# A three-layer graph attention kernel: tiles of nodes taken from the last to the first, and dense pieces placed between the edge steps

## The chip, the cores and the metric

The kernel runs on one core of one Trainium2 chip. The metric is device time in microseconds (us) of one execution, smaller is better. The engines that matter are TensorE (PE, with its weight loads as PEld), VectorE (DVE), ScalarE (ACT), GpSimd (POOL), and the queue of SyncE (SP) for plain DMAs.

## What is computed

There are 4096 nodes with 512 features, and an adjacency matrix of 4096 x 4096 zeros and ones. Its chance of an edge falls with both node numbers, as 1/sqrt((i+1)(j+1)), so the first nodes have many edges and the last few. The reference, shortened:

```python
def gat(x, mask, W, a):                 # heads of one layer
    Wh = einsum('nf,hfo->hno', x, W)
    e = leaky_relu(src(Wh, a)[:, :, None] + dst(Wh, a)[:, None, :], 0.2)
    e = where(mask, e, -huge)
    return einsum('hnm,hmo->hno', softmax(e), Wh)

x  = layernorm(x + gat(x, mask, W0, a0))          # layer 0, 8 heads of 64
h  = elu(gat(x, mask, W1, a1))                    # layer 1, 8 heads of 64
h  = elu(gat(h, mask, Wo, ao))                    # layer 2, 1 head of 512
h  = relu(h @ lin1_w + lin1_b) @ lin2_w + lin2_b  # dense, 512 -> 1024 -> 512
out = layernorm(x + h)
```

All arithmetic is in float32.

## The kernel before

Nodes are cut into 32 tiles (`NT`) of 128 (`P`). The kernel first searches the edges of each tile and packs them, in `find_edges`: the result is, per tile, a number of chunks of 128 edges. Each half of a tile (64 nodes) has chunks of its own, so that a pair of chunks serves both halves. Beside the search, `beside` projects the tile for layer 0. The chunk counts are fixed when the program is built: tile 0 has 55 (in four parts), tile 1 has 22, then 17, 15, 14, 12, 12, 11, four tiles of 10, ten of 8, one of 7, and tiles 23 to 31 have 6. That is 339 in all, 284 without tile 0.

A layer reads a table in DRAM with one row per node: 512 projected features and the scores of its heads. `attend(pools, st, t)` walks over the chunks of one tile in steps of up to `GC = 3` pairs. A step does this:

- one gather on POOL for each chunk (L880, indirect DMA of 128 rows into the tile `g`);
- the nodes' own scores by a matmul with the packed selection (pss, L890), summed by DVE into `s` (L898);
- `z` from `s` and the gathered scores, leaky relu, less the part for the shift (L904 to L908, DVE);
- weights by two exponentials on ACT (`w`, L910, and `wp` in PSUM, L916);
- in layers 0 and 1, the gathered rows times `wp` in place (L918, DVE), and a 0/1 selection `sm` (L919); in layer 2 one `sm` per chunk that holds the weight (L927);
- matmuls on PE that add the rows up by node (`acc`) and the weights (`den`), L939.

Buffers: `g` has six steps in layers 0 and 1 and four in layer 2; `acc` has two, `den` one, `pss` two in layers 0 and 1 and one in layer 2.

In `heads_layer` (layers 0 and 1) `after(sums, t)` finishes a tile: `o` is acc over den (L977), then `finish` (layer 0: residual, layernorm, row stored; layer 1: elu), then `project` makes the rows of the next layer's table: transposes `pt` (L631), copy to `xt` (ACT, L633), the sums `xpart` (DVE, L638) that are added to `xsum` on POOL (L639), the product `ph` (L642) and the scores `pa` (L645), and the row written out (`hrow`, L622 and L623, stored by SP). `project_end` closes the table with a row for nodes without edges, so the first gather of the next layer comes after the last projection. The loop goes over tiles 0 to 31, and `after` of a tile stands behind the whole `attend` of the next one.

Layer 2 has `fold` in place of `after` (acc over den, elu, transposes, a column of `sht`, L1047 to L1057). Four tiles make a block (`NJ = 4`). `first_dense(b, ks)` does two of eight slices of the first dense layer of a block (L1065, ACT relu L1068), `second_dense(b, j)` the second dense layer and the layernorm of one tile (p2, L1077, one PSUM buffer; L1080, L955 to L961) and stores it. In each turn of the loop over t, after the `fold` of tile t-1, the kernel does one piece of `first_dense` of the block before and one `second_dense` of the block before that.

The order of the instructions on each engine isn't the order of the text. The tile framework puts them in order when the program is built, with the order of the text as the priority and its own estimates of when operands are ready; it also places the waits. Each engine then works through its own list.

Of the kernel before, what the change touches and what calls it, by code (L numbers as in the profile page):

```python
# [24 lines left out]
NT = N // P  # L25
NB = 512
NBLK = N // NB
NJ = NB // P
# [4 lines left out]
HC = HID // P  # L33
# [6 lines left out]
GC = 3  # L40
# [489 lines left out]
def sparse_path(  # L530
# [24 lines left out]
    pts = parts()  # L555
# [39 lines left out]
    st0 = Stage2("t0", 8, 64, dest_first=False)  # L595
# [29 lines left out]

    def project(sb, ps, st, proj, src, t, smalls=1):
        w_sb, wa = proj
# [5 lines left out]
        nc.scalar.copy(xt, pt)  # L633
        if t == 0:
            nc.vector.tensor_reduce(st.xsum, xt, AX.X, OP.add)
        else:
            part = sb.tile([P, FC], F32, name="xpart")
            nc.vector.tensor_reduce(part, xt, AX.X, OP.add)  # L638
            nc.gpsimd.tensor_add(st.xsum, st.xsum, part)  # L639
# [222 lines left out]

    def attend(pools, st, t):

        gp, wk, pacc, ps = pools
        hs = st.heads
        acc = pacc.tile([P, F], F32, name="acc")
        den = pacc.tile([P, hs], F32, name="den", bufs=1)
        runs = []
        for p in pts:  # L870
            if p.t == t:
                small = min(p.chunks)
                for a, b, hn in ((0, small, 2), (small, p.pairs, 1)):
                    runs += [(p.first + lo, min(GC, b - lo), hn) for lo in range(a, b, GC)]
        seen, left = [0, 0], [sum(m for _, m, hn in runs if hn > h) for h in range(2)]
        for c0, m, hn in runs:
# [19 lines left out]
            n = m * hn  # L896
# [33 lines left out]
            for i in range(m):  # L930
# [3 lines left out]
                for out_, rows in (  # L934
# [3 lines left out]
                    for h in range(hn):  # L938
# [5 lines left out]
                        )  # L944
        return acc, den

# [16 lines left out]
    def heads_layer(st, nxt, proj_of, finish):  # L963
        with ExitStack() as pools:
# [6 lines left out]
            ps = pools.enter_context(tc.tile_pool(name=f"hp_{st.name}", bufs=1, space=PSUM))  # L971
            def after(sums, t):
                acc, den = sums
                o = sb.tile([P, F], F32, name="o")
# [8 lines left out]
                finish(sb, o, t)  # L983
                project(sb, ps, nxt, proj, o, t, 2)


            acc = attend((gp, wk, pacc, ps), st, 0)
            for t in range(1, NT):
                ahead, acc = acc, attend((gp, wk, pacc, ps), st, t)
                after(ahead, t - 1)  # L990
            after(acc, NT - 1)
            project_end(sb, ps, nxt, proj, 2)
# [12 lines left out]
    with ExitStack() as pools:  # L1005
# [7 lines left out]
        def beside(t):  # L1013
            xr = sb.tile([P, F], F32, name="xr")
            nc.sync.dma_start(xr, x[ts(t, P), :])
            project(sb, ps, st0, proj, xr, t)

# [8 lines left out]
    with tc.tile_pool(name="tb", bufs=1) as big, tc.tile_pool(name="tg", bufs=4) as gp, \  # L1026
# [14 lines left out]
        nc.sync.dma_start(l2b, lin2_b.partition_broadcast(P))  # L1041
        hts, hids = {}, {}

        def fold(sums, t):
            acc, den = sums
            rd = sb.tile([P, 1], F32, name="rd")
# [5 lines left out]
            for c in range(FC):  # L1052
                nc.tensor.transpose(pt[:, c, :], o[:, ts(c, P)], ident)
            b, j = divmod(t, NJ)
            if j == 0:
                hts[b] = big.tile([P, FC, NB], F32, name="sht", bufs=2)
            nc.scalar.copy(hts[b][:, :, ts(j, P)], pt)  # L1057

        def first_dense(b, ks):
# [10 lines left out]
        def second_dense(b, j):  # L1070
            t = b * NJ + j
            xr = sb.tile([P, F], F32, name="xr")
# [12 lines left out]

        acc = None
        for t in range(NT + 2 * NJ + 1):
            ahead, acc = acc, attend((gp, wk, pacc, ps), st, t) if t < NT else None
            if ahead is not None:
                fold(ahead, t - 1)  # L1090
            b, j = divmod(t - 1, NJ)
            if 1 <= b <= NBLK:
                first_dense(b - 1, range(j * HC // NJ, (j + 1) * HC // NJ))
            if 2 <= b:
                second_dense(b - 2, j)

# [55 lines left out]
```

## Time and profile before

| what | value |
|---|---|
| three runs, us | 2890.80, 2912.05, 2925.34; median 2912.05 |
| profiled execution, us | 2625.14, span 2623.2 |
| mean granted TensorE clock | 0.849 |
| edge search, with layer 0's projection | 0 to 692 us of the span |
| layer 0 | 692 to 1300 |
| layer 1 | 1300 to 1855 |
| layer 2 | 1855 to 2623 |
| gathers | 1017, POOL busy 1.01 us each |
| HBM traffic | 371.00 MB read, 42.23 MB written |

The profiled execution is one run by itself with the hardware profiler on. Every stage and duration comes from it, and it is shorter than the three runs. Rows of the profile name a line of the kernel, the engine, the operation, and the tiles written and read. "Busy" is the time in which an engine has an instruction at work; the granted clock is the share of the full clock that PE was given.

### The profile page before, as it was taken

Reading aid. Unit: us, or ns where it says so; the run is one execution under the profiler, and the core shown is the slowest. Engines: PE = TensorE matmul, PEld = TensorE weight load, DVE = VectorE, ACT = ScalarE, POOL = GpSimd, SP = SyncE. Lnnn points to the kernel's source line nnn. Section 1 sums busy time; section 2 is a strip of 40 time slices with the busy share of each in tenths; the row PEclk is TensorE's granted clock in tenths of the full one; section 3 lists DMA queues with packets and bytes.
Section 4 is the critical chain, followed back from the end, with each engine's and each line's share of the span. In section 5 each row is a group of like instructions: output and inputs, shape, how many; then the busy total and the mean of one; then the engine's idle time right before and its main releaser. Section 6 shows DMA issues by size and latency. Waiting matters only on the chain.

```text
span 2623.2 us, 28047 instructions
## 1 busy us (share of the span) xinstructions
PE 2001.1 (76%) x8501; PEld 891.6 (34%) x8501; DVE 1617.4 (62%) x5141; ACT 509.5 (19%) x919; POOL 1082.8 (41%) x1276
## 2 busy tenths in 40 slices
PE   2125788999467777777647777887567899999997
PEld 0002333334123333333312333443233444444443
DVE  5998777888666777766556777776234334443322
ACT  1001223333001222222101111222000123232320
POOL 3000000000177775563067776771577744453000
PEclk9556668999678888888867898999787999999999
DMA  5002244654277886674167787782677754454111
GB/s 172 0 33 80 95 151 161 227 200 180 70 204 236 244 247 190 198 237 143 68 172 205 217 219 193 202 220 79 210 201 202 201 155 146 139 164 132 57 36 46
DMA packets 138071, 415.21 MB, mean 158 GB/s; under 512 B 33515, under 2 KB 33523, under 8 KB 133814
## 3 DMA queue, kind: packets, MB, share of 16 engines
q0 software_dynamic: 81360, 269.62, 36.9%
q1 hardware_dynamic: 56550, 143.70, 15.5%
q8 instruction: 70, 1.15, 0.2%
q14 instruction: 91, 0.75, 0.1%
HBM read 371.00 MB, written 42.23 MB: 158 GB/s over the span
## 4 chain that ended last, share of the span: by engine, by line
PE 50%; DVE 22%; DMA 9%; issue 8%; POOL 7%; ACT 2%; POOLq 0%; SPq 0%; DVEq 0%; ACTq 0%
PE ph L642 13%; PE acc L939 11%; DMA g<-table_t,idx 8%; PE p L1065 8%; PE p L1077 8%; POOL g L880 6%; DVE g L918 5%; DVE cand L737 4%; PE pa L645 3%; PE key L731 2%; PE key L730 2%; DVE cand L754 1%; PE pt L631 1%; DVE lst L752 1%; ACT xt L633 1%
## 5 line engine op out<-in xcount | busy, mean ns | idle before, releaser
L880 POOL DMA_INDIRECT g<-table_t,idx x1017 | 1027.4, 1010 | 569.8 <-issue 278.0
L939 PE MATMUL acc<-g,sm 128*64 128x512 f32 x2034 | 618.9, 703 | 141.4 <-DVE g L918 127.6
L642 PE MATMUL ph<-sw_t,xt 128*128 128x512 f32 x768 | 456.2, 727 | 46.1 <-ACT xt L633 46.1
L918 DVE TENSOR_TENSOR g<-g,wp 128x3072 f32<-128x3072 f32 (+4 forms) x156 | 384.4, 2464 | 14.5 <-ACT wp L916 14.2
L939 PEld LDWEIGHTS acc<-g,sm 128*64 128x64 f32 x2034 | 159.0, 157 | 359.2 <-issue 150.6
L1065 PE MATMUL p<-sht,sl1w 128*128 128x512 f32 x512 | 234.4, 601 | 0.7 <-ACT sht L1057 0.7
L642 PEld LDWEIGHTS ph<-sw_t,xt 128*128 128x128 f32 x768 | 158.3, 227 | 216.9 <-issue 150.4
L1077 PE MATMUL p<-sl2w,shid 128*128 128x512 f32 x512 | 225.4, 593 | 3.7 <-DVE xr L1080 3.7
L639 POOL TENSOR_TENSOR xsum_t<-xsum_t,xpart 128x4 f32<-128x4 f32 x93 | 20.3, 218 | 487.4 <-DVE xpart L638 312.7
L737 DVE MAX8 cand<-key 128x8 f32<-128x353 f32 (+55 forms) x467 | 204.3, 447 | 22.2 <-PE key L731 21.9
L904 DVE TENSOR_TENSOR z<-s,g 128x48 f32<-128x48 f32 (+8 forms) x234 | 42.3, 184 | 220.5 <-DMA g<-table_t,idx 217.2
L721 ACT ACTIVATE sg<-raw 128x4096 bf16<-128x4096 int32 x32 | 115.7, 3617 | 218.8 <-PE key L730 211.5
L910 ACT ACTIVATE w<-z 128x48 f32<-128x48 f32 (+8 forms) x234 | 50.2, 220 | 522.3 <-DVE z L908 504.3
L730 PE MATMUL key<-sg,s_identb 128*128 128x512 bf16 (+1 forms) x258 | 114.2, 443 | 48.2 <-DVE cand L737 19.3
L1077 PEld LDWEIGHTS p<-sl2w,shid 128*128 128x128 f32 x512 | 97.0, 190 | 127.5 <-issue 120.5
L622 ACT COPY hrow<-ph 128x512 f32<-128x512 f32 (+1 forms) x99 | 57.8, 584 | 379.1 <-PE ph L642 331.4
L1065 PEld LDWEIGHTS p<-sht,sl1w 128*128 128x128 f32 x512 | 91.7, 190 | 93.3 <-issue 91.9
L645 PEld LDWEIGHTS pa<-swa_t,xt 128*128 128x128 f32 x768 | 108.4, 209 | 42.6 <-issue 30.5
L757 POOL COPY over<-lst 128x1 f32<-128x1 f32 x35 | 6.5, 187 | 275.6 <-DVE lst L752 247.4
L890 PE MATMUL pss<-s_t,s 128*128 128x48 bf16 (+1 forms) x543 | 49.0, 181 | 87.3 <-DVE s L898 82.2
L939 PEld LDWEIGHTS den<-w,sm 128*64 128x64 f32 x1356 | 67.5, 149 | 138.9 <-ACT w L910 63.9
L731 PE MATMUL key<-frac,ones_b 64*128 64x512 bf16 (+1 forms) x258 | 114.6, 444 | 0.0
(132 smaller groups left out, 2240.3 us busy)
## 6 DMA issues: line engine op xcount, KB each, us to landing
raw<-in_adj_dram SPq DMA_DIRECT2D x32, 2048.0 KB, 8.0
table_t<-hrow SPq DMA_DIRECT2D x64, 260.0 KB, 2.1
xr<-in_x_dram SPq DMA_DIRECT2D x64, 256.0 KB, 4.4
g<-table_t,idx POOLq DMA_INDIRECT x1017, 4.0
table_t<-hrow SPq DMA_DIRECT2D x32, 256.5 KB, 4.3
sx_d<-o SPq DMA_DIRECT2D x32, 256.0 KB, 4.5
xr<-sx_d SPq DMA_DIRECT2D x32, 256.0 KB, 2.6
out_dram<-xr SPq DMA_DIRECT2D x32, 256.0 KB
```

The lines of the kernel that those rows point to most:

```text
L622: nc.scalar.copy(hrow[:n, :F], ph[:n].rearrange("p h d -> p (h d)"))
L642: nc.tensor.matmul(ph, xt[:, c, :], w_sb[:, c], start=(c == 0), stop=(c == FC - 1))
L645: nc.tensor.matmul(pa, xt[:, c, :], wa[:, c], start=(c == 0), stop=(c == FC - 1))
L721: nc.scalar.activation(sg, raw, AF.Sign)
L730: nc.tensor.matmul(key[:, j - w0_ : e - w0_], ident_b, sg[:, j:e], start=True, stop=False)
L731: nc.tensor.matmul(key[:, j - w0_ : e - w0_], ones_b, frac[:, j:e], start=False, stop=True)
L737: nc.vector.max(out=cand[:, at : at + 8], in_=part)
L880: nc.gpsimd.indirect_dma_start(out=g[:, i, h, :], out_offset=None, in_=st.table[:, :], in_offset=bass.IndirectOffsetOnAxis(ap=idx[:, c0 + ...
L918: nc.vector.tensor_mul(body, body, wp[:, :, :, None].to_broadcast([P, n, hs, st.dim]))
L939: nc.tensor.matmul(out_[h * HN : (h + 1) * HN], sm[:, i * hn + h], rows[h], start=first[h], stop=seen[h] == left[h],)
L1065: nc.tensor.matmul(p1, l1w[:, c, ts(k, P)], hts[b][:, c, :], start=(c == 0), stop=(c == FC - 1))
L1077: nc.tensor.matmul(p2, hids[b][:, k, ts(j, P)], l2w[:, k, :], start=(k == 0), stop=(k == HC - 1))
```

## The change

Five things change.

1. `attend` becomes a generator that yields after each step, with the number of gathers in it; it leaves `acc` and `den` in a dictionary.
2. A tile's steps get even sizes: pairs are cut into equal parts rather than threes and a rest. The number of steps stays 78. Four pairs become 2+2 in place of 3+1.
3. In layers 0 and 1 the tiles go from 31 to 0, and `after` of the tile before comes behind the first step of a tile, not behind its last. The first tile of the order, and not tile 0, sets `xsum`.
4. In layer 2 the order is 31, 30, 29, 28, 27, 0, 26, ... 1. Blocks are made of four tiles that follow each other in this order; the first has 24 gathers.
5. Dense pieces go into a list when the last tile of their block is folded: four pieces of `first_dense` and four of `second_dense`. From the second block on, each gather adds 64/315 to what is due, and after a step as many pieces are done as are due and ready. What is left is done at the end.

```diff
--- before.py
+++ after.py
@@ -623,7 +623,7 @@
         nc.vector.tensor_copy(hrow[:n, F:], pa[:n, 1, :])
         nc.sync.dma_start(st.table[lo : lo + n, :], hrow[:n, :])
 
-    def project(sb, ps, st, proj, src, t, smalls=1):
+    def project(sb, ps, st, proj, src, t, first, smalls=1):
         w_sb, wa = proj
         hs, dm = st.heads, st.dim
         pt = ps.tile([P, FC, P], F32, name="pt")
@@ -631,7 +631,7 @@
             nc.tensor.transpose(pt[:, c, :], src[:, ts(c, P)], ident)
         xt = sb.tile([P, FC, P], F32, name="xt")
         nc.scalar.copy(xt, pt)
-        if t == 0:
+        if first:
             nc.vector.tensor_reduce(st.xsum, xt, AX.X, OP.add)
         else:
             part = sb.tile([P, FC], F32, name="xpart")
@@ -860,18 +860,27 @@
         nc.vector.tensor_copy(flag, pf[:1])
 
 
-    def attend(pools, st, t):
-
-        gp, wk, pacc, ps = pools
-        hs = st.heads
-        acc = pacc.tile([P, F], F32, name="acc")
-        den = pacc.tile([P, hs], F32, name="den", bufs=1)
+    def runs_of(t):
+
         runs = []
         for p in pts:
             if p.t == t:
                 small = min(p.chunks)
                 for a, b, hn in ((0, small, 2), (small, p.pairs, 1)):
-                    runs += [(p.first + lo, min(GC, b - lo), hn) for lo in range(a, b, GC)]
+                    steps = math.ceil((b - a) / GC)
+                    cuts = [a + (b - a) * i // steps for i in range(steps + 1)] if steps else []
+                    runs += [(p.first + i, j - i, hn) for i, j in zip(cuts, cuts[1:])]
+        return runs
+
+    def attend(pools, st, t, sums):
+
+
+        gp, wk, pacc, ps = pools
+        hs = st.heads
+        acc = pacc.tile([P, F], F32, name="acc")
+        den = pacc.tile([P, hs], F32, name="den", bufs=1)
+        sums[t] = acc, den
+        runs = runs_of(t)
         seen, left = [0, 0], [sum(m for _, m, hn in runs if hn > h) for h in range(2)]
         for c0, m, hn in runs:
             g = gp.tile([P, GC, 2, st.row], F32, name="g")[:, :m, :hn]
@@ -942,7 +951,7 @@
                             rows[h],
                             start=first[h], stop=seen[h] == left[h],
                         )
-        return acc, den
+            yield n
 
     def elu(sb, t):
         ex = sb.tile([P, F], F32, name="ex")
@@ -969,8 +978,10 @@
             sb = pools.enter_context(tc.tile_pool(name=f"hs_{st.name}", bufs=2))
             pacc = pools.enter_context(tc.tile_pool(name=f"ha_{st.name}", bufs=2, space=PSUM))
             ps = pools.enter_context(tc.tile_pool(name=f"hp_{st.name}", bufs=1, space=PSUM))
-            def after(sums, t):
-                acc, den = sums
+            sums = {}
+
+            def after(t):
+                acc, den = sums.pop(t)
                 o = sb.tile([P, F], F32, name="o")
                 rd = sb.tile([P, HS], F32, name="rd")
                 nc.vector.reciprocal(rd, den)
@@ -981,14 +992,18 @@
                     op=OP.mult,
                 )
                 finish(sb, o, t)
-                project(sb, ps, nxt, proj, o, t, 2)
-
-
-            acc = attend((gp, wk, pacc, ps), st, 0)
-            for t in range(1, NT):
-                ahead, acc = acc, attend((gp, wk, pacc, ps), st, t)
-                after(ahead, t - 1)
-            after(acc, NT - 1)
+                project(sb, ps, nxt, proj, o, t, t == order[0], 2)
+
+
+
+            order = list(range(NT - 1, -1, -1))
+            ahead = None
+            for t in order:
+                for step, _ in enumerate(attend((gp, wk, pacc, ps), st, t, sums)):
+                    if step == 0 and ahead is not None:
+                        after(ahead)
+                ahead = t
+            after(ahead)
             project_end(sb, ps, nxt, proj, 2)
 
     def finish0(sb, o, t):
@@ -1013,7 +1028,7 @@
         def beside(t):
             xr = sb.tile([P, F], F32, name="xr")
             nc.sync.dma_start(xr, x[ts(t, P), :])
-            project(sb, ps, st0, proj, xr, t)
+            project(sb, ps, st0, proj, xr, t, t == 0)
 
         find_edges(big, sb, ps, pk, constants, beside)
         project_end(sb, ps, st0, proj)
@@ -1039,10 +1054,15 @@
         nc.vector.tensor_copy(l1b, pb)
         l2b = big.tile([P, F], F32, name="sl2b")
         nc.sync.dma_start(l2b, lin2_b.partition_broadcast(P))
-        hts, hids = {}, {}
-
-        def fold(sums, t):
-            acc, den = sums
+
+
+        order = list(range(NT - 1, 0, -1))
+        order.insert(NJ + 1, 0)
+        blocks = [order[i : i + NJ] for i in range(0, NT, NJ)]
+        hts, hids, sums, ready = {}, {}, {}, []
+
+        def fold(t):
+            acc, den = sums.pop(t)
             rd = sb.tile([P, 1], F32, name="rd")
             nc.vector.reciprocal(rd, den)
             o = sb.tile([P, F], F32, name="o")
@@ -1051,10 +1071,14 @@
             pt = ps.tile([P, FC, P], F32, name="pt")
             for c in range(FC):
                 nc.tensor.transpose(pt[:, c, :], o[:, ts(c, P)], ident)
-            b, j = divmod(t, NJ)
+            b, j = divmod(order.index(t), NJ)
             if j == 0:
                 hts[b] = big.tile([P, FC, NB], F32, name="sht", bufs=2)
             nc.scalar.copy(hts[b][:, :, ts(j, P)], pt)
+            if j == NJ - 1:
+                per = HC // NJ
+                ready.extend((first_dense, b, range(i * per, (i + 1) * per)) for i in range(NJ))
+                ready.extend((second_dense, b, i) for i in range(NJ))
 
         def first_dense(b, ks):
             if 0 in ks:
@@ -1068,7 +1092,7 @@
                 nc.scalar.activation(hids[b][:, k, :], p1, AF.Relu, bias=l1b[:, k : k + 1])
 
         def second_dense(b, j):
-            t = b * NJ + j
+            t = blocks[b][j]
             xr = sb.tile([P, F], F32, name="xr")
             nc.sync.dma_start(xr, x1_d[ts(t, P), :])
             nc.vector.tensor_add(xr, xr, l2b)
@@ -1083,16 +1107,23 @@
 
 
 
-        acc = None
-        for t in range(NT + 2 * NJ + 1):
-            ahead, acc = acc, attend((gp, wk, pacc, ps), st, t) if t < NT else None
-            if ahead is not None:
-                fold(ahead, t - 1)
-            b, j = divmod(t - 1, NJ)
-            if 1 <= b <= NBLK:
-                first_dense(b - 1, range(j * HC // NJ, (j + 1) * HC // NJ))
-            if 2 <= b:
-                second_dense(b - 2, j)
+        head = sum(sum(p.chunks) for p in pts if p.t in blocks[0])
+        rate_ = 2 * NT / (sum(sum(p.chunks) for p in pts) - head)
+        due, ahead = 0.0, None
+        for t in order:
+            for step, chunks in enumerate(attend((gp, wk, pacc, ps), st, t, sums)):
+                if step == 0 and ahead is not None:
+                    fold(ahead)
+                if t not in blocks[0]:
+                    due += chunks * rate_
+                while due >= 1 and ready:
+                    due -= 1
+                    piece, *what = ready.pop(0)
+                    piece(*what)
+            ahead = t
+        fold(ahead)
+        for piece, *what in ready:
+            piece(*what)
 
 
 @with_exitstack
```

## The prediction, made before the changed kernel ran

> **What bounds the kernel now.** I read the page's busy shares first, then a table of stages (windows cut where the gathers of each layer begin), then the timeline of one repeating period in layers 0 and 1. No engine is full over the span, so the stages have to be read one by one.
>
> ```profile
> span 2623.2 us, 28047 instructions
> PE 2001.1 (76%) x8501; PEld 891.6 (34%) x8501; DVE 1617.4 (62%) x5141; ACT 509.5 (19%) x919; POOL 1082.8 (41%) x1276
> ...
> L880 POOL DMA_INDIRECT g<-table_t,idx x1017 | 1027.4, 1010 | 569.8 <-issue 278.0
> ```
> ```profile
> 0.00:692.00 692.00, 463.12 (x1422) 186.84 (x1423) 560.37 (x2395) 153.24 (x97) 41.70 (x197) 0.74 0.35 124
> 692.00:1300.00 608.00, 440.36 (x2198) 200.67 (x2195) 402.53 (x898) 111.99 (x284) 349.25 (x370) 0.82 0.65 194
> 1300.00:1855.00 555.00, 416.27 (x2208) 186.66 (x2206) 371.11 (x801) 85.18 (x255) 351.14 (x371) 0.87 0.68 186
> 1855.00:2095.00 240.00, 167.07 (x883) 90.16 (x885) 92.99 (x429) 24.59 (x69) 183.99 (x183) 0.85 0.72 207
> 2095.00:2623.20 528.20, 514.32 (x1803) 227.26 (x1798) 190.43 (x618) 134.53 (x214) 156.71 (x156) 0.99 0.38 110
> ```
> Columns: window, length, busy us and instructions of PE, PEld, DVE, ACT, POOL, granted clock, DMA share, GB/s. Row 1 is the edge search, which the change leaves as it is. Rows 2 and 3 are layers 0 and 1. Rows 4 and 5 are layer 2: 240 us paced by gathers while PE works 167, then PE without a gap.
>
> A gather takes POOL 1.00 us and 0.30 us of issue, 1.30 us in a row; a layer has 339 of them, 441 us. Layers 0 and 1 last longer than that, and PE (440, 416) and DVE (403, 371) don't fill them either. What sets the small tiles is a chain that goes round between the engines. Layer 0, tiles of eight gathers:
>
> ```profile
> 1057.98 0.69 DVE L977 TENSOR_TENSOR o<-acc,rd 128x512 f32<-128x512 f32 x1 [0.82 <-PE acc L939]
> ...
> 1060.31 1.11 PE L631 MATMUL pt<-s_ident,o 128*128 128x128 f32 x4 [2.41 <-DVE o L961]
> ...
> 1061.46 0.59 ACT L633 COPY xt<-pt 128x512 f32<-128x512 f32 x1 [4.27 <-PE pt L631]
> ...
> 1062.10 5.36 PE L642 MATMUL ph<-sw_t,xt 128*128 128x512 f32 x8 [0.68 <-ACT xt L633]
> ...
> 1068.18 0.64 PE L631 MATMUL pt<-s_ident,o 128*128 128x128 f32 x4
> ...
> 1068.45 0.65 DVE L898 TENSOR_REDUCE s<-pss 128x48 f32<-128x144 f32 x2
> ...
> 1069.50 2.84 PE L642 MATMUL ph<-sw_t,xt 128*128 128x512 f32 x6 [0.65 <-ACT xt L633]
> ...
> 1071.14 3.35 DVE L918 TENSOR_TENSOR g<-g,wp 128x3072 f32<-128x3072 f32 x1 [0.33 <-ACT wp L916]
> ```
> Two tiles share one turn. Two projections (ph, L642) stand close together, and the second runs on PE while DVE goes on with the scores. In the chain that ended last, ph x8 returns at 1062.10 and 1090.71: 28.6 us for two tiles, 14.3 each. In layer 1 two such tiles take 24.3 us (the 3.36 us steps of L918 at 1631.66 and 1656.02), 12.15 each. Pairs of six gathers take 27.3 (1231.71 to 1259.05) and 20.1 us (1777.09 to 1797.16).
>
> **What the skill says.** "TensorE: Matmul & The Clock Gate", Part 1: an idle window of some 3.4 us halves PE's clock and a busy one restores it. The trace agrees: eight ph matmuls took 6.14 us after a wait at 1203.88, but a matmul in a run costs 0.43, so 3.44 for eight; the clock granted in layer 0 was 0.82. The same page, on the queues: only weight loads are pulled ahead on PE, matmuls stay in program order, and DVE and ACT are strict first-in first-out. In the timeline I saw no instruction overtake another there. So the order in which the built program places instructions decides what can overlap, and I compared that order of both kernels.
>
> **The change, part by part.** Search: same order, 0 us. The steps get more even sizes (eight gathers: 4+4 for 6+2), 78 steps as before: 0. `first`: the same operations under another tile, 0.
>
> *Layers 0 and 1: the turn is no longer shared.* `after` now comes after the first step of the next tile. For the 22 tiles of 7 gathers and more (22 to 1), the changed program's order on PE is this, once per tile (number of matmuls):
> ```
> den 4, acc 4 (end of tile T) | den 4, acc 4 (start of the next) | pt 4, ph 4, pa 4 (projection of T) | pss 2, pss 2
> ```
> and on DVE: both s reductions and z, g times wp twice, o<-acc of T, residual and norm, xpart, then hrow<-pa, then the next s. The next s stands behind hrow, which waits for pa; pt waits for o, which waits for both products. Nothing of one tile's turn overlaps the next tile's. I add up its links from the timeline of before:
> - s to product: 2.7 us (1068.45 to 1071.14), of which 0.5 was a table load behind the xt copy; 2.2.
> - products: 3.348/6 = 0.56 us per gather.
> - wait for acc's last matmuls: 0.2, up to 0.8 on the slow clock.
> - o to pt in layer 0: 4.2 (o at 1226.93, o<-o,mv,sd at 1230.52 plus 0.55). Layer 1, with elu for the norm: 2.95 (1643.10 to 1645.29 plus 0.69 and the handover).
> - pt to ph: 1.3 (1210.75 to 1212.06) to 1.8 (1060.31 to 1062.10).
> - ph to next s: 3.44+0.96+0.23 and 0.4 of handover = 5.0; slow 7.1 (1203.88 to 1211.02).
>
> Fast sums for n gathers: layer 0 13.0+0.56n, layer 1 11.7+0.56n (rounded). PE now idles some 4.5 us in each turn (s to product, then the first product), beyond the window above, so I add 1.7 in layer 0 and 1.2 in layer 1 (where the clock was higher); bounds 0 and 2.7. For n=8: 19.2 against 14.3, and 17.4 against 12.15. The extra gather distance doesn't help: eight gathers are 10.4 us.
>
> Sum of layer 0: the nine tiles of six gathers (31 to 23) keep the shared turn, 4.5 x 27.3 = 123. Tiles 22 to 1 have 230 gathers: 22 x 14.7 + 0.56 x 230 = 452. Tile 0 (55 gathers, 16 steps): on POOL its last 31 gathers stand behind the xsum addition of tile 1 (L639), so 7 until xpart, 31 x 1.3 = 40, 4 to land, 9 for the last step: 60. Together 635, from the first z at 721.7: 1357. The last projection then adds 10.5+1.7, to 1369. Before, the last ph began at 1294.03 and pa was done by 1299: **+70** (bounds 44 and 92).
>
> Layer 1: 90 + 22 x 12.9 + 129 + 60 = 563, from the first z at 1330.6: 1894, plus 9.2: 1903, against 1842 (last ph 1836.59 plus 5.40): **+61** (34 and 94). The wait that goes, small tiles left over after the last gather (1205 to 1298), is paid for in these sums: gathers no longer decide before tile 0.
>
> *Layer 2.* Full-clock prices: a block's dense work 64 x 0.43 x 2 = 55 us; a gather's acc, den and pss on PE 0.64 (a period of 19.6 us with eight gathers, less 13.7 dense and 0.7 for pt). From the first gather (1854.9), in PE's new order: 30 gathers until block 0 is ready, paced by POOL, 44; block 0's dense work with 37 gathers of tile 0, 79; 37 gathers up to block 1's, partly fetched, 27; blocks 1 to 5 with 24, 28, 32, 30 and 45 gathers, 73, 77, 80, 77, 88; block 6 with 68 gathers, the last 45 short of dense work, 107; block 7 alone with its tail, 70. That is 722, so an end at 2577 against 2623: -46. Against it: second_dense now follows second_dense with one p2 buffer, 1.2 us each (8.08 apart at 2581.56 and 2589.64, for 6.87): three per block, 25 us, of which acc matmuls fill half. **-30** (-50 to 0). Its idle start shrinks, but 681 us of PE work remain.
>
> Sum: 70+61-30 = +101 against the profiled execution (2625.1 us, span 2623.2), 2726, or 3.9%. The three runs have a median of 2912.05, 287 us above that execution, and nothing in the trace says where; I keep between the same ratio (3024) and the same difference (3013): **3020**. A change of about 1% is the least that a measurement of this kernel tells from none.
>
> **Rivals.**
> 1. *The turns still overlap* (faster). If DVE's waits close up, DVE's work is the price: 4.1 a tile plus 0.95 per gather, 11.7 for n=8, below 14.3. Then layer 0 is 123+308+60, -74 with its start and end, layer 1 -55, layer 2 -30: -159, about 2745. It decides from an eight-gather turn under 14.3 us (12.15 in layer 1). For it: DVE is idle for a third of both layers. Against: the order above, where each engine's next instruction waits for the one just placed elsewhere. Chance 0.12.
> 2. *Balanced*: turns only 1 to 2 us longer (22 x 1.5 x 2 = 66) and layer 2 at its better end, -50: +16, about 2930. For it: layer 2's idle 240-167 us is plain. Chance 0.06.
> 3. *Slow clock throughout*: both layers at their upper bounds and tile 0 slower: +186 and layer 2 at 0, then block bursts that starve POOL (four g buffers), 20 more: +206, about 3130. For it: clock 0.80 in the six-gather turns. Chance 0.15.
>
> **Numbers.** Forecast 0.67. Slower 0.67+0.15 = 0.82, same 0.06, faster 0.12. The range 2915 to 3120 leaves out rival 1 and part of rival 3.
>
> **What would show it.** Right: in layers 0 and 1 the turn of an eight-gather tile is 17 to 20 and 16 to 19 us with one ph x8 each; POOL waits in the middle of both layers instead of their end; layers 0 and 1 grow 40 to 95 us each, and layer 2 shrinks by 0 to 50. Wrong: turns under 14 us, two projections per turn, or layer 2 shorter by over 80.

## The result, and the profile after

The changed kernel takes 3111.77 us (median of four runs, 3102.29 to 3117.39) against 2917.21 for the kernel before: ratio 1.068, 95% interval 1.0603 to 1.0757. It is slower, as forecast, and 92 us above the forecast of 3020, near the upper end of its range (2915 to 3120).

The kernel before took 2620 us in the first set of runs below (and 2625 in the profiled execution shown above), but 2914 in the second and third set and 2917 beside the changed kernel; nothing in the kernels explains this, so a time is compared only inside its set, and traces only with the same time of the kernel before.

The page of the changed kernel begins:

```profile
span 3115.4 us, 27990 instructions
PE 2133.2 (68%) x8477; PEld 932.7 (30%) x8501; DVE 1627.2 (52%) x5141; ACT 549.7 (18%) x945; POOL 1089.8 (35%) x1276
...
L889 POOL DMA_INDIRECT g<-table_t,idx x1017 | 1035.3, 1018 | 1191.5 <-PE acc L948 431.3
```

The same line in a trace of the kernel before that has about the same time as its median (2904.2 us, `before_ref` of the third set):

```profile
L880 POOL DMA_INDIRECT g<-table_t,idx x1017 | 1033.5, 1016 | 755.4 <-issue 292.0
```

The gathers (now L889) cost what they did, 1.02 us each. What grew is POOL's idle time before them, from 755.4 to 1191.5 us, and its main releaser is now PE's acc, 431.3 us, where it was POOL's own issue. So the gathers wait for buffers that acc has not yet freed.

The stages of the changed kernel, cut at the first gather of each layer (window, length, busy us of PE, PEld, DVE, ACT, POOL, clock, DMA share, GB/s):

```profile
0.00:710.30 710.30, 455.28 (x1407) 186.62 (x1431) 574.42 (x2424) 153.82 (x98) 41.73 (x198) 0.74 0.35 124
710.30:1510.10 799.80, 483.31 (x2193) 213.92 (x2193) 412.80 (x892) 145.48 (x308) 349.04 (x370) 0.76 0.50 147
1510.10:2228.30 718.20, 465.32 (x2199) 207.60 (x2199) 364.88 (x778) 86.48 (x254) 350.59 (x371) 0.79 0.50 142
2228.30:3115.40 887.10, 729.33 (x2678) 324.61 (x2678) 275.08 (x1047) 163.94 (x285) 348.46 (x339) 0.89 0.42 122
```

The stages of the kernel before in `before_ref` (span 2902.3):

```profile
0.00:719.30 719.30, 464.58 (x1413) 190.13 (x1437) 574.16 (x2425) 153.87 (x98) 41.86 (x198) 0.73 0.35 122
719.30:1433.10 713.80, 459.25 (x2193) 206.12 (x2194) 401.23 (x892) 113.02 (x285) 350.28 (x370) 0.79 0.56 165
1433.10:2088.70 655.60, 454.32 (x2190) 200.19 (x2189) 359.44 (x777) 82.92 (x253) 355.11 (x370) 0.80 0.56 155
2088.70:2902.30 813.60, 690.54 (x2681) 313.02 (x2681) 280.92 (x1047) 159.01 (x283) 341.26 (x339) 0.91 0.47 133
```

Row by row: search -9.0, layer 0 +86.0, layer 1 +62.6, layer 2 +73.5; together +213, the whole difference of the spans. The forecast had 0, +70, +61 and -30. Three rows agree roughly; the fourth has the wrong sign. (The search's length varies from 705 to 720 between kernels with the same search.)

One turn of an eight-gather tile in layer 0 of the changed kernel, from its timeline:

```profile
1062.05 3.70 PE L642 MATMUL ph<-sw_t,xt 128*128 128x512 f32 x8 [0.67 <-issue]
...
1066.58 0.17 DVE L623 COPY hrow<-pa 128x8 f32<-128x8 f32 x1 [3.80 <-PE ph L642]
...
1067.58 0.26 DVE L907 TENSOR_REDUCE s<-pss 128x32 f32<-128x96 f32 x1 [0.76 <-PE pss L899]
...
1071.27 2.29 DVE L927 TENSOR_TENSOR g<-g,wp 128x2048 f32<-128x2048 f32 x1 [0.26 <-ACT wp L925]
...
1073.82 2.29 DVE L927 TENSOR_TENSOR g<-g,wp 128x2048 f32<-128x2048 f32 x1
...
1077.36 0.69 DVE L988 TENSOR_TENSOR o<-acc,rd 128x512 f32<-128x512 f32 x1 [1.26 <-PE acc L948]
...
1077.60 1.02 POOL L889 DMA_INDIRECT g<-table_t,idx  x1 [7.82 <-PE acc L948]
...
1081.51 0.66 PE L631 MATMUL pt<-s_ident,o 128*128 128x128 f32 x4 [1.99 <-DVE sd L969]
```

Read down it: projection on PE while DVE waits 3.8 us, then the scores and products on DVE while PE waits, then o, then pt of the next projection. There is one ph x8 per turn, and next to nothing of two tiles lies side by side: only the acc matmuls of the next tile's first step run beside the norm of o. POOL stands 7.82 us before it may fetch. The next ph began at 1082.84. From the o of tile 22 to that of tile 12 the ten eight-gather tiles take 19.8 us each in layer 0 and 18.7 in layer 1; in `before_ref` they take 16.2 and 14.9 (tile 11 to tile 21).

Layer 2, two neighbouring kinds of window in the changed kernel:

```profile
2378.00:2428.00 50.00, 31.07 (x147) 12.87 (x146) 16.47 (x77) 3.45 (x12) 35.79 (x36) 0.74 0.68 197
2428.00:2478.00 50.00, 41.91 (x117) 18.65 (x117) 11.95 (x51) 10.87 (x20) 7.49 (x7) 0.85 0.16 45
2478.00:2528.00 50.00, 41.89 (x172) 18.41 (x170) 21.55 (x68) 8.96 (x16) 18.92 (x19) 0.90 0.45 131
2528.00:2578.00 50.00, 46.83 (x132) 20.83 (x129) 8.45 (x34) 10.08 (x16) 10.07 (x10) 0.93 0.19 54
2578.00:2628.00 50.00, 35.52 (x160) 16.66 (x159) 19.88 (x71) 10.36 (x18) 26.63 (x27) 0.86 0.60 174
```

PE and POOL take turns. 36 gathers in one window and 7 in the next, while PE is 31 us busy and then 42. In layer 2 of before, PE worked almost without a gap for the last 528 us (514 us busy, in the first trace and in `before_ref`). The waits of POOL in layer 2 (total, times, longest):

```profile
POOL g L889 <- PE den L948: 218.6, 22, 48.4
```

In `before_ref`:

```profile
POOL g L880 <- PE den L939: 137.3, 19, 10.0
```

The longest wait went from 10.0 to 48.4 us, which is seven dense pieces at the forecast's 6.87 us each.

### The profile page after: what moved, and what is told of

Same layout as the page of the kernel before. It is cut to its first block, busy times and chain, and to the rows that moved or that the text cites. A ratio compares the mean times of both kernels' runs of the same rounds, so it can differ in the third digit from the quotient of the medians.

```text
span 3115.4 us, 27990 instructions
## 1 busy us (share of the span) xinstructions
PE 2133.2 (68%) x8477; PEld 932.7 (30%) x8501; DVE 1627.2 (52%) x5141; ACT 549.7 (18%) x945; POOL 1089.8 (35%) x1276
## 5 line engine op out<-in xcount | busy, mean ns | idle before, releaser
L889 POOL DMA_INDIRECT g<-table_t,idx x1017 | 1035.3, 1018 | 1191.5 <-PE acc L948 431.3
L948 PE MATMUL acc<-g,sm 128*64 128x512 f32 x2034 | 695.7, 767 | 166.0 <-DVE g L927 129.4
L642 PE MATMUL ph<-sw_t,xt 128*128 128x512 f32 x768 | 470.1, 753 | 56.0 <-ACT xt L633 38.7
L927 DVE TENSOR_TENSOR g<-g,wp 128x3072 f32<-128x3072 f32 (+2 forms) x156 | 385.0, 2468 | 27.0 <-ACT wp L925 18.2
L948 PEld LDWEIGHTS acc<-g,sm 128*64 128x64 f32 x2034 | 171.5, 171 | 404.7 <-issue 244.0
L948 PE MATMUL den<-w,sm 128*64 128x8 f32 x1356 | 82.3, 222 | 167.2 <-ACT w L919 101.5
L623 DVE COPY hrow<-pa 128x8 f32<-128x8 f32 (+3 forms) x99 | 15.9, 161 | 279.3 <-PE pa L645 155.2
L948 PEld LDWEIGHTS den<-w,sm 128*64 128x64 f32 x1356 | 83.1, 172 | 256.4 <-issue 143.9
L631 PE MATMUL pt<-s_ident,o 128*128 128x128 f32 x256 | 47.0, 312 | 156.7 <-DVE o L970 89.6
L907 DVE TENSOR_REDUCE s<-pss 128x48 f32<-128x144 f32 (+8 forms) x234 | 53.5, 230 | 161.4 <-remote 76.6
L1104 DVE TENSOR_TENSOR xr<-p,xr 128x512 f32<-128x512 f32 x32 | 22.0, 689 | 209.1 <-PE p L1101 176.5
```

The costliest lines, as they stand in the source:

```text
L642: nc.tensor.matmul(ph, xt[:, c, :], w_sb[:, c], start=(c == 0), stop=(c == FC - 1))
L889: nc.gpsimd.indirect_dma_start(out=g[:, i, h, :], out_offset=None, in_=st.table[:, :], in_offset=bass.IndirectOffsetOnAxis(ap=idx[:, c0 + ...
L907: nc.vector.tensor_reduce(s, pss[:, :m].rearrange("p m g a h -> p (m g) h a")[:, :: 3 - hn], AX.X, OP.add,)
L927: nc.vector.tensor_mul(body, body, wp[:, :, :, None].to_broadcast([P, n, hs, st.dim]))
L948: nc.tensor.matmul(out_[h * HN : (h + 1) * HN], sm[:, i * hn + h], rows[h], start=first[h], stop=seen[h] == left[h],)
```

## The experiments

### First set: which layer, and which part of it

The kernel before took 2620.24 us here (seven runs). The totals expected for this set took a before of 2912 to 2917 us, so only differences from before can be compared with them.

`before_again` is the kernel before without an edit, to see whether a profiled execution is faster than the others.

> The kernel before, profiled once more. The profiled execution of before (2625 us) was 290 us shorter than its timed ones (2917), while that of the changed kernel (3117) agrees with its own (3112). Theory A (chance): this one lasts about 2915 us, and its stages show where the 290 us lie. Theory B (the profiler shortens this kernel): 2625 us again.

Measured: 2619.7 us, span 2617.7, stages 707.0, 608.0, 534.6 and 768.1. Timed and profiled executions agree inside this set; so the 287 us between the median and the profiled execution, which the forecast had to carry along, are no matter of the profiler.

`heads_only`: layers 0 and 1 as changed; layer 2 with its old order and loop.

```diff
-        order = list(range(NT - 1, 0, -1))
-        order.insert(NJ + 1, 0)
+        order = list(range(NT))
...
+            if 1 <= b <= NBLK:
+                first_dense(b - 1, range(j * HC // NJ, (j + 1) * HC // NJ))
+            if 2 <= b:
+                second_dense(b - 2, j)
```

> Layers 0 and 1 as in the changed kernel, layer 2 in the old tile order with the old dense loop. Theory S (the shared turn is lost in layers 0 and 1): slower than before by 120 to 230 us, so 3040 to 3150. Theory L2 (the loss lies in layer 2): within 40 us of before, 2880 to 2960.

Measured: 2811.65 us, ratio 1.0725 (1.0682 to 1.0769), +191, inside the 120 to 230 of theory S. Stages:

```profile
708.90:1420.80 711.90, 476.94 (x2193) 209.69 (x2193) 411.88 (x892) 145.48 (x308) 349.48 (x371) 0.79 0.56 165
1420.80:2045.90 625.10, 433.31 (x2196) 195.08 (x2197) 364.81 (x778) 86.59 (x254) 353.64 (x370) 0.85 0.58 163
2045.90:2814.20 768.30, 685.11 (x2681) 315.81 (x2680) 282.63 (x1047) 158.68 (x283) 343.20 (x339) 0.95 0.48 140
```

Layer 0 +103.9, layer 1 +90.5, layer 2 as before, although its steps are cut evenly here. The eight-gather turns (tile 22 to tile 12) are 19.1 and 17.4 us, the forecast's own 19.2 and 17.4.

`l2_only`: layer 2 as changed; layers 0 and 1 in the old order with `after` behind the whole next tile. The even cuts stay in all layers.

```diff
-            order = list(range(NT - 1, -1, -1))
+            order = list(range(NT))
...
-                for step, _ in enumerate(attend((gp, wk, pacc, ps), st, t, sums)):
-                    if step == 0 and ahead is not None:
-                        after(ahead)
+                for _ in attend((gp, wk, pacc, ps), st, t, sums):
+                    pass
+                if ahead is not None:
+                    after(ahead)
```

> Layer 2 as in the changed kernel (with the even steps everywhere), layers 0 and 1 from tile 0 up with after behind the whole next tile. Theory S: 2870 to 2930, a little under before. Theory L2: 3040 to 3120.

Measured: 2719.41 us, ratio 1.0384 (1.0345 to 1.0423), +99. Neither theory had this: S had this kernel a little under before, L2 about 120 to 200 us above it. Both parts of the change lose. Stages 617.9, 558.6 and 834.0: the even cuts alone cost 10 and 24 us in layers 0 and 1, and layer 2 is 66 us longer. A run of its windows shows a lump whole:

```profile
2045.00:2085.00 40.00, 30.50 (x128) 13.86 (x128) 18.79 (x79) 6.92 (x17) 27.70 (x28) 0.83 0.66 193
2085.00:2125.00 40.00, 40.00 (x110) 17.48 (x109) 7.02 (x16) 5.70 (x10) 0.73 (x1) 1.00 0.08 27
2125.00:2165.00 40.00, 33.40 (x140) 14.81 (x138) 17.69 (x70) 9.73 (x18) 24.53 (x24) 0.91 0.65 184
```

For 40 us PE works without a gap while POOL issues one gather; in the windows around it PE idles for 9.5 and 6.6 of 40 us and its mean clock is 0.83 and 0.91.

`rev_late`: the changed kernel, layers 0 and 1 from the last tile to the first, but `after` behind the whole next tile (the second half of the edit above, without the first).

> The changed kernel, but in layers 0 and 1 after stands behind the whole next tile again; the tiles still go from 31 to 0. The built order on PE shows two projections per turn again. Theory S (place of after): the loss of layers 0 and 1 goes, 2850 to 2930. Rival O (the order of tiles makes the loss, with the large tile last): 3080 to 3120, as the changed kernel.

Measured: 2670.69 us, ratio 1.0196 (1.0159 to 1.0233), +50. Stages 593.2, 536.5 and 834.0: layers 0 and 1 have lost nothing, and the +50 comes from layer 2, 66 us longer, which the expectation left out. Rival O is out. Against `heads_only`, with the same order and cuts, the place of `after` alone is 118.7 us in layer 0 and 88.6 in layer 1. Against `l2_only` the reversed order alone is worth 25 and 22 us here.

### Second set: the place alone, the cuts, the pieces

The kernel before took 2914.01 us here (31 runs).

`after_again` is the changed kernel without an edit.

> The changed kernel unaltered, on the chip of the other runs, where the kernel before takes 2620 us. Theory of sums: the parts seen so far add up: search 707, layers 0 and 1 as in the run with the heads alone changed (712 and 625), layer 2 as in the run with layer 2 alone changed (834): 2878 us, ratio 1.098. Rival: the ratio of the first measurement (1.068) holds on every chip, 2799 us; then a part of the two losses is shared between them.

Measured: 3103.14 us, ratio 1.063 (1.057 to 1.069), stages 707.4, 795.6, 718.7 and 883.4. This set has the pace of the first measurement, so it repeats that ratio and tests neither theory: the whole change was never measured where before takes 2620 us. The parts of the first set can't be added up for this one; an eight-gather turn of layer 0 in before takes 16.2 us at this pace (`before_ref`), not 14.3.

`early_fwd`: the place without the reversed order. Layers 0 and 1 in the old tile order, `after` behind the first step; layer 2 old, by the edit of `heads_only`; even cuts.

```diff
-            order = list(range(NT - 1, -1, -1))
+            order = list(range(NT))
```

> Layers 0 and 1 in the old tile order (0 to 31) with even steps, and only the place of the projection as in the change: behind the first step of the next tile. Layer 2 in its old form. Theory S (the place breaks the shared turn, whatever the tile order): layer 0 about 735 us (618 with the late place), layer 1 about 645 (559), layer 2 768, total about 2859, ratio 1.09; one ph x8 per turn. Rival R (the loss needs the reversed order): layers 0 and 1 at 620 and 560, total about 2655, ratio 1.013.

Measured: 3020.09 us, ratio 1.0346 (1.0289 to 1.0404).

```profile
708.20:1500.40 792.20, 489.07 (x2193) 213.85 (x2194) 412.62 (x892) 143.66 (x307) 350.03 (x370) 0.76 0.50 148
1500.40:2222.30 721.90, 452.48 (x2191) 203.06 (x2191) 365.63 (x777) 84.89 (x253) 349.89 (x370) 0.80 0.51 141
2222.30:3029.60 807.30, 693.52 (x2681) 316.63 (x2680) 281.29 (x1047) 158.85 (x283) 343.12 (x339) 0.92 0.47 134
```

Layers 0 and 1 are as long as in `after_again` (795.6, 718.7) within 4 us, with the tiles in the old order. The loss doesn't need the reversed order: rival R is out. The sizes expected were those of the other set. `l2_even`, further down in this set, has the same order and cuts in layers 0 and 1 and only the place late:

```profile
719.50:1440.10 720.60, 454.07 (x2193) 203.55 (x2194) 401.11 (x892) 116.33 (x287) 351.63 (x370) 0.80 0.55 163
1440.10:2129.10 689.00, 460.79 (x2194) 201.28 (x2193) 361.32 (x777) 81.62 (x253) 351.82 (x371) 0.80 0.55 148
```

So the place costs 72 us in layer 0 and 33 in layer 1 here. The even cuts in the old order put `l2_even` 7 and 33 us above before of the third set, so in layer 1 the cuts bring about as much as the place.

`rev_oldcuts`: reversed order, late `after` and old layer 2 by the edits of `rev_late` and `heads_only`, and steps cut as before:

```diff
-                    steps = math.ceil((b - a) / GC)
-                    cuts = [a + (b - a) * i // steps for i in range(steps + 1)] if steps else []
-                    runs += [(p.first + i, j - i, hn) for i, j in zip(cuts, cuts[1:])]
+                    runs += [(p.first + lo, min(GC, b - lo), hn) for lo in range(a, b, GC)]
```

> Layers 0 and 1 from the last tile to the first with the projection behind the whole next tile, steps cut in the old way (3+1 pairs, not 2+2), layer 2 in its old form. If the even cuts cost under either order what they cost in the old one (10 us in layer 0, 24 in layer 1): layer 0 583, layer 1 513, layer 2 768, total 2571, ratio 0.981: faster than before. Rival: with the reversed order the cuts cost nothing: 593 and 537, total 2605, ratio 0.994.

Measured: 2925.02 us, ratio 1.0025 (0.9993 to 1.0057). Stages 729.1, 665.4 and 809.2: 15 and 10 us more than before in the third set. Neither expected ratio (0.981, 0.994) came. The reversed order gained 47 us in the first set, with even cuts, and gains nothing in this one, with old cuts. Whether it is the cuts or what makes the sets differ stays open.

`l2_even`: the kernel of `l2_only`, with the pieces of a block spread over the gathers of the next.

```diff
-        head = sum(sum(p.chunks) for p in pts if p.t in blocks[0])
-        rate_ = 2 * NT / (sum(sum(p.chunks) for p in pts) - head)
+        rates = {}
+        for blk in blocks[1:]:
+            gathers = sum(sum(p.chunks) for p in pts if p.t in blk)
+            rates.update((t, 2 * NJ / gathers) for t in blk)
...
-                    due += chunks * rate_
+                    due += chunks * rates[t]
```

> Layers 0 and 1 in the old order with even steps and the late projection; layer 2 as changed, but the eight pieces of a block are spread evenly over the gathers of the block behind it, so that no debt of due pieces builds up while none is ready. Theory L (bursts of pieces starve the gathers, and then PE waits for gathers): layer 2 at 765 us or less instead of 834, total 2650 or less, ratio to before at most 1.012; the prediction's sum for layer 2 (738) would give 2623. Rival M (tile order, early fold and pieces between steps hold up acc and the buffers of g even without bursts): layer 2 stays above 815, total above 2700.

Measured: 2907.92 us, ratio 0.9976 (0.9954 to 0.9999).

```profile
2129.10:2908.70 779.60, 687.14 (x2678) 309.89 (x2678) 281.30 (x1047) 174.47 (x293) 347.14 (x339) 0.96 0.48 138
```

Layer 2 takes 779.6 us, 104 less than in `after_again` and 34 less than before in the third set. Tile order, early fold and pieces between the steps are all still there. Rival M is out: the lumps are the cause, and without them the stage gains about what the forecast gave it. The total expected was again that of the first set; layers 0 and 1 (720.6 and 689.0) have the even cuts.

### Third set: where the lumps come from, and a faster version

The kernel before took 2913.66 us here (37 runs).

`before_ref` is the kernel before, for its stages (shown with the result).

> The kernel before, unaltered, for its stages on the chip of the other runs of this call: if DMA landings are what differs between the chips (stores of hrow and gathers land later there), layer 2, which is bound by PE for 528 of its 768 us, grows little (up to 810 us) and layers 0 and 1, whose turns contain landings, grow by over 100 us each; if PE's clock alone differs, all stages grow by one ratio, the edge search too.

Measured: stages 719.3, 713.8, 655.6 and 813.6, against 707.0, 608.0, 534.6 and 768.1 in the first set: +12, +106, +121 and +46. These are about the sizes expected of late DMA landings, not one ratio for all stages. PE's busy time grew by 21, 43 and 7 us in the three layers, so PE working more slowly in what the trace records covers only a part. In layers 0 and 1 some 330 us of waits end in an event that the trace names only "remote", where the first set's trace has none of that name. By the trace's semaphore events, all of them end when PE's own semaphore rises, more than 1.5 us after the last end of a matmul that the trace records. One of them:

```profile
1066.69 1.92 PE L939 MATMUL acc<-g,sm 128*64 128x512 f32 x8
...
1074.94 0.56 DVE L919 TENSOR_TENSOR sm<-iota_n,nl 128x384 f32<-128x384 f32 x1 [5.48 <-remote]
...
1078.05 1.11 PE L631 MATMUL pt<-s_ident,o 128*128 128x128 f32 x4 [9.44 <-DVE bs L955]
```

The last matmul ends at 1068.61, and PE's semaphore rises for the last time at 1074.91. So these waits are for results of PE that come late, not for DMA landings. Added up from the last recorded end to the last rise before PE's next matmul, wherever it is over 1.5 us, such stretches take 94, 86 and 44 us in the three layers of `before_ref`, up to 12.9 us each. `before_again` has none, but for the end of the program, which is left out in both. That is 224 of the 285 us between the two traces. Why PE is late there isn't shown. The record gives the chip the number 13 in the first and in the third set and 8 in the second, so the pace doesn't go with that number.

`l2_zero_last`: the kernel of `l2_only` with its one rate, but tile 0 last.

```diff
-        order = list(range(NT - 1, 0, -1))
-        order.insert(NJ + 1, 0)
+        order = list(range(NT - 1, -1, -1))
```

> Layer 2 as changed, with its one rate of pieces for the whole layer, but tile 0 last (31 to 0) instead of sixth; layers 0 and 1 in the old order with even steps and the late projection. Theory D (the debt comes from tile 0's place: 73 gathers in block 1 make some 15 pieces due where only 8 are ready, and later blocks are then issued whole): the pieces come one by one and layer 2 takes 760 to 800 us instead of 834 (883 on the slower chip): total at least 35 us below the one with tile 0 sixth. Rival (any order descending with the early fold is slow): layer 2 within 15 us of that with tile 0 sixth.

Measured: 2900.92 us, ratio 0.9966 (0.9948 to 0.9984). Layer 2 takes 772.1 us; from its middle:

```profile
2332.00:2382.00 50.00, 50.00 (x203) 22.22 (x200) 25.01 (x90) 15.28 (x24) 22.10 (x22) 1.00 0.52 149
2382.00:2432.00 50.00, 50.00 (x196) 22.15 (x195) 20.31 (x79) 13.74 (x23) 26.98 (x27) 1.00 0.55 148
2432.00:2482.00 50.00, 48.03 (x205) 23.04 (x204) 21.99 (x74) 13.26 (x23) 28.86 (x29) 1.00 0.66 184
```

PE is full, its clock is 1.00, and POOL issues 22 to 29 gathers in each window. Layer 2 is inside the expected 760 to 800 us. Moving one tile removed the lumps, so theory D holds. The sum behind it: the rate is 64 pieces for 339 - 24 = 315 gathers, 0.203 per gather. With tile 0 sixth, block 1 has 73 gathers, so 14.8 pieces fall due, while only the eight of block 0 are ready. The other 6.8 stay due, and when block 1 is folded its pieces come all at once. The built order on PE shows both (number of matmuls, den left out; eight of p1 or p2 are one piece; the traces record each of these matmuls twice):

```
tile 0 sixth: ... pss 16, acc 18, pss 12, ... acc 1, p1 32, p2 8, acc 2, p2 8, acc 2, p2 8, acc 1, pt 4, acc 1, p2 8
tile 0 last:  ... p1 4, pss 2, pt 4, p1 2, acc 4, p1 6, pss 2, p1 2, acc 4, p1 6, pss 2, pt 4, p2 2, acc 4, p2 6
```

In the first line a stretch of tile 0 has no dense work, and then eight pieces (55 us at 6.87 each) have a handful of acc matmuls between them. Four buffers of at most six gathers hold 24, 31 us of POOL's work.

`best_rev` and `best_fwd`: `l2_even` with the old cuts; layers 0 and 1 reversed in the one, in the old order (as in before) in the other.

> Layers 0 and 1 from the last tile to the first, projection behind the whole next tile, old cuts; layer 2 in the changed tile order with the pieces spread evenly over each block; old cuts there too. From the parts: layer 2 gives 28 us (780 for 808), the reversed order in layers 0 and 1 gives between 0 (as seen on one chip) and 47 us (on the other): ratio 0.972 to 0.990, faster than before. If the gain in layer 2 needed the even cuts: 0.985 to 1.003.

> As the other version with evenly spread pieces and old cuts, but layers 0 and 1 in the old order, so that they are those of the kernel before, and only layer 2 differs: if even spreading in layer 2 is worth 28 us, ratio 0.990; if the reversed order in layers 0 and 1 is worth something, this one is slower than the reversed one by up to 47 us.

Measured: `best_rev` 2893.53 us, ratio 0.9928 (0.9903 to 0.9953), layers 0 and 1 732.7 and 664.3, layer 2 788.8. `best_fwd` 2872.24 us, ratio 0.989 (0.9846 to 0.9934):

```profile
709.60:1423.80 714.20, 452.03 (x2193) 204.21 (x2194) 401.31 (x892) 112.85 (x285) 350.95 (x371) 0.79 0.56 165
1423.80:2091.10 667.30, 453.95 (x2193) 201.12 (x2192) 358.61 (x777) 82.63 (x253) 354.51 (x370) 0.80 0.55 152
2091.10:2864.00 772.90, 680.27 (x2678) 306.39 (x2678) 281.81 (x1047) 175.10 (x293) 344.58 (x339) 0.95 0.49 140
```

Layer 2 is 41 us shorter than before; layer 1, whose code is that of before, 12 us longer in this execution. This version beats both kernels, the one before by 1.1% (0.7 to 1.5), as expected (0.990). The reversed order brings nothing on top: `best_rev` is 18 us longer in layer 0, 3 shorter in layer 1, and 16 longer in layer 2, where both have the same code; the two intervals overlap, so which of them is better isn't settled. One stage with one code comes out up to 16 us apart in these executions, so the 15 and 10 us of `rev_oldcuts` and the 7 us of layer 0 in `l2_even` show nothing by themselves.

## Why the prediction was right, and where it was not

**The shared turn is lost: right.** The forecast read it from the order on PE and DVE and summed a serial turn to 19.2 and 17.4 us for eight gathers; measured are 19.8 and 18.7 in the changed kernel, 19.1 and 17.4 in `heads_only`. One ph x8 per turn, POOL waiting in the middle of the layers: both seen. `early_fwd` and `rev_late` show that the place of `after` does it, in both tile orders.

**Layers 0 and 1, +70 and +61: right on this measurement (+86, +63), in part by luck, and too low in the first set (+104, +90).** What was lost per eight-gather tile here is 3.6 and 3.9 us, not 4.9 and 5.25, because the turn of before is longer too. (The 12.15 us of layer 1 was one pair of tiles; the ten tiles took 12.7 each in that trace.) The luck is in two things that the forecast had at nothing. The +61 was meant for the place of `after`, which alone costs 33 us in layer 1 at this pace, and the even cuts come on top. And the stretches in which PE's results come late take 34 us less in layers 0 and 1 of the changed kernel (81 and 64) than in `before_ref` (94 and 86); without them the two layers would be 98 and 84 us longer than before, as in the first set. Two terms were too small in both sets:

- Tile 0, forecast 60 us: from the o of tile 1 to that of tile 0 it took 74 and 72 in `heads_only`, and 86 and 80 in the changed kernel. The 31 gathers behind the xsum addition of tile 1 were right. But in layer 0 of `heads_only` that addition comes 12.8 us after the o of tile 1 (1313.1), not 7, and after one more gather POOL waits for acc again, 5.8 us, which the sum had not:

```profile
1325.88 0.50 POOL L639 TENSOR_TENSOR xsum_t<-xsum_t,xpart 128x4 f32<-128x4 f32 x1
1326.53 1.02 POOL L889 DMA_INDIRECT g<-table_t,idx  x1
1333.32 1.06 POOL L889 DMA_INDIRECT g<-table_t,idx  x1 [5.78 <-PE acc L948]
```

- Turns of ten gathers and more. The wait for acc was taken as 0.2, up to 0.8; in the tiles of ten it is 2.7 to 3.0:

```profile
1093.10 0.69 DVE L988 TENSOR_TENSOR o<-acc,rd 128x512 f32<-128x512 f32 x1 [2.73 <-PE acc L948]
...
1115.93 0.69 DVE L988 TENSOR_TENSOR o<-acc,rd 128x512 f32<-128x512 f32 x1 [2.96 <-PE acc L948]
```

The turn between these two is 22.8 us, where the forecast's formula gives 14.7 + 5.6 = 20.3; the other three turns of ten gathers take 20.9 to 21.2. The 22 turns of layer 0 took 470 us in `heads_only`, forecast 452: 18 us here and 14 of tile 0 make up 32 of the 34 by which that run exceeds the forecast.

**Even cuts at nothing: wrong in the old order.** They cost 10 and 24 us in `l2_only`; only the 24 is clear of the spread between executions. Equal numbers of steps were taken for equal cost. In the changed kernel, where the turn is serial, their share was not tried alone.

**Layer 2, -30 (-50 to 0): wrong, +73.5.** This is the step that failed, and most of the miss: with -30 there the changed kernel would have spanned 3012 us. The stage's length was about right for work that is spread: `l2_even` and `l2_zero_last` come to -34 and -41. But the sum counted how many pieces are ready, not how many are due, and so missed the 6.8 pieces carried over. It let the dense work of each block lie beside the gathers that follow, and it priced the second half of tile 0, where no piece is ready, by PE's work: 27 us for 37 gathers "partly fetched". In the changed kernel this stretch, from the last p2 of block 0 to the first p1 of block 1, lasts 68.9 us (2376.1 to 2445.0), and 50.5 in `l2_only`; 37 gathers in a row are 48. The lumps stood in the third rival, priced at 20 us; they cost 104 (`after_again` against `l2_even`).

Part of these 104 us goes with PE's clock. PE is busy for 722 us of layer 2 in `after_again` (clock 0.90) and for 687 in `l2_even` (0.96), with the same matmuls: 35 of the 104. The Trainium skill, "TensorE: Matmul & The Clock Gate", Part 1, has a reason for it: an idle window halves the clock until a busy one restores it. The trace agrees: where PE never waits (`l2_zero_last`, 2332 to 2432) the clock stands at 1.00. The rest of the 104 is time without recorded work of PE. Some 41 us of it are stretches in which PE's results come late (70 and 29 us); whether the lumps bring these on isn't shown. The first set's traces have no such stretches, and there layer 2 of `l2_only` is still 66 us longer than that of before.

**The scale.** The forecast kept between the same ratio and the same difference to pass from 2625 to 2912 us. `before_ref` shows that neither is how it goes: 227 of the 285 us lie in layers 0 and 1. It did little harm.

**Slips that changed little.** The forecast's rows for layers 0 and 1, like the table of stages before it, begin at 692 and 1300 us; the first gathers of these layers are at 711.3 and 1320.3, so layer 1 lasted 535 us and not 555. Its sums use the times of z and ph and are not touched by this. The gathers in its sum for layer 2 add up to 331 of 339; the other eight are 5 us at its 0.64 each.

**The rivals.** Turns that overlap (1) and balance (2) are out. The total is near rival 3's 3130, but not by its sizes: layers 0 and 1 lie near the forecast's values, and the lumps alone are five times as dear as it had them.

## What to carry to other kernels

Where each engine works through its list in order, the place of a tile's finishing work decides whether two tiles can share a turn; compare the built order of both versions before adding up work. When side work is paced by a credit per step, sum the credit against what is ready at each point: credit that builds up while nothing is ready comes back as a lump, and a lump longer than the buffers cover stops the transfers and then the engine that waits for them. Judge a change that joins several edits stage by stage: here one of them, the dense pieces between the steps, is a gain of 25 to 41 us in its stage (`best_rev`, `l2_even`, `best_fwd`, `l2_zero_last`) that a single tile's place turned into a loss.

## What the runs showed of the hardware

The same program took 2620 us in one set of runs and 2904 to 2914 in others. The work of DVE and POOL does not differ: DVE is busy for 1617 and 1616 us, POOL for 1090 and 1089. PE is busy for 1986 and 2069 us, at a clock of 0.853 and 0.811. The larger part of the difference, 224 of 285 us, is made of stretches of up to 12.9 us in which PE records no matmul and then reports a result (`before_ref`). The traces of the second and third set and that of the changed kernel have them, those of the first set don't, and nothing here shows their cause.

The loss of the changed kernel depends on the set: an eight-gather turn of layer 0 went from 14.3 to 19.1 us in the first set and from 16.2 to 19.8 in the others. The stretches go with a part of that: they take 180 us of layers 0 and 1 before the change and 145 after it. Where PE's semaphore rises long after its last recorded matmul, a trace's word "remote" can hide the core's own PE.
